# Row tiles and two banks per product in layer 1's first-support stages of a two-layer graph network, with its per-node weights in bursts of two pairs

## The chip, the core and the metric

The kernel runs on one core of a Trainium2 chip. The core has a matrix engine (TensorE, PE in the profile, whose weight loads have a row PEld), a vector engine (VectorE, DVE), a scalar engine (ScalarE, ACT), GpSimd (POOL) and SyncE (SP). Each engine takes its own instructions in program order. TensorE writes only into PSUM, which has eight banks of 512 fp32 values in each of 128 partitions; VectorE and ScalarE read the results from there into SBUF. DMAs are issued from SP, POOL and ACT. The metric is device time in microseconds: the median of three runs, beside one execution taken by the hardware profiler.

## The reference

Two layers, one after the other, on x of shape (8, 2048, 64) with one 2048 x 2048 matrix `adj`; both add a graph convolution to x and normalise over the 64 channels.

```python
# layer 0: supports I, A, 2 A A - I
w = einsum('nd,dkio->nkio', embedding, weight);  b = einsum('nd,do->no', embedding, bias)
x_g = einsum('knm,bmc->bnkc', A_stack, x)
x = layernorm(x + einsum('bnki,nkio->bno', x_g, w) + b)
# layer 1: supports I, A, 2 A A - I, and a fourth made from the embeddings E
apt = softmax(relu(E @ E.T), axis=1)
x_g = einsum('knm,bmc->bknc', stack([I, A, 2*A@A - I, apt]), x)
x = layernorm(x + einsum('bnki,nkio->bno', x_g, weights) + E @ bias_pool)
```

So every node has its own weights, made from a 16-long embedding. All is fp32. The kernel writes an embedding as two parts (a rounded value and what is left), so that a product over 16 embedding rows is one over 64 rows of fast-format (`F32R`) values.

## The kernel before

Nodes are cut into 8 blocks of 256. The work is 40 stages, five phases of eight blocks: A0 and B0 (layer 0: u = A x, then A u with the output), A1 (layer 1: u = A x, the stages that the change is about, numbers 16 to 23), Z1 (softmax support, 24 to 31) and V1 (A u and the output, 32 to 39). The batch and channels of a node make 512 columns.

**Products.** A stage's main work is a product over 2048 rows. Block 0 of A1 is made in the plain way (`straight`, L484): 32 matmuls of 128 contracting rows and 512 columns, 16 for each of two 128-row slabs, two accumulators of one bank each. Blocks 1 to 7 use Strassen's seven products (`strassen`, L504), in the order 1, 4, 7, 2, 6, 5, 3, each of 8 matmuls of 128 rows x 256 columns. An fp32 matmul is two instructions in the profile. Each product has one bank of two in turn (`accumulator`, L480). As a product ends, VectorE adds it to others (L575 to L616); products 1 and 4 are first copied by ScalarE. One matmul of 256 columns counts as one step: a Strassen stage has 56 steps, the plain one 64.

**Everything else is put between the steps.** `put(n, place, job)` plans a job of stage n at a place between 0 and 64, scaled by 56/64 in a stage of 56 steps (L820); the loop from L949 issues a step of the product, then every job that has come due. So order on each engine is fixed by these places. In A1 they are (L886 to L893, L900 to L917):

- `turn(1)` of the block before, at 4: eight transposes of its finished u into one two-bank tile, then four copies by ScalarE;
- `weights` of the block before, in six bursts from 12 to 36 (L336): matmuls of 64 contracting rows (`wst` by `e2`), always two row tiles that work on the two halves h of the array's rows, each with its own bank. Four bursts of six pairs and two of four, two pairs to a two-bank tile. The tiles are then copied to `w`, by ScalarE, but one of each burst by VectorE (L366):

```python
on_dve = k == (0 if self.phase == "V1" else len(made) // 2) and v not in spare and self.n and (v > 16 if self.phase == "A0" else self.phase != "V1" or v0)
```

- `store_c` of the block before, at 24;
- `scores_of_rows` (s=0: two halves, at 38 and 40; s=1: at 57 and 60): two matmuls of 512 columns into one two-bank tile, one VectorE reduction of 1024 columns; `statistics` after each two: small VectorE work and two ScalarE exponentials of 1024 columns. For block 0, s=1 goes into the next stage (14.2 and 19);
- `bias` at 38.5: two small matmuls, then two VectorE additions of 512 columns;
- `apply` of the block before, four times at 43: 32 matmul instructions each in four column tiles of 32, then four VectorE multiply-adds of 256 columns;
- `turn(0, "x")` at 47 (57 in block 0): the same eight transposes for x; two copies by VectorE and two by ScalarE.

All these take a two-bank PSUM tile from `big` (L96), three in turn. With the two accumulators that is all eight banks. Stage 16 also has the tail of layer 0's last block: its `apply` and normalisation, and VectorE's sums of x for Strassen (`sums["A1"].make` at 20, 24 and 32; the fourth in stage 17 at 10). Weights for block 7 of A1 are made in stage 24.

The score matmuls of Z1 (`scores`, `numerators`) contract over 128 rows of `e2`, whose two halves hold the same 64 rows; the upper half of `s1` and `bst` is zero.

SP's queue loads `adj` tiles (four buffers) and `wst` tiles (three), and stores u (L499). POOL's queue stores and loads the rest.

Of the kernel before, what the change touches and what calls it, by code (L numbers as in the profile page):

```python
# [9 lines left out]
F32 = mybir.dt.float32  # L10
F32R = mybir.dt.float32r
AF = mybir.ActivationFunctionType
ALU = mybir.AluOpType
# [35 lines left out]
def two_graph_layers(ctx: ExitStack, tc: tile.TileContext, x, x_t, adj_b, adj_q, layers, out):  # L49
# [33 lines left out]
    ps_acc = ctx.enter_context(tc.tile_pool(name="ps_acc", bufs=1, space=PSUM))  # L83
    ps_big = ctx.enter_context(tc.tile_pool(name="ps_big", bufs=3, space=PSUM))

    in_use = [0]
    in_turn = mybir.DependencyInfo(mybir.DependencyClass.Sync, mybir.DependencyReason.DATA)

    def acc_bank(i):

        return ps_acc.tile([P, BC], F32, tag=f"acc{in_use[0] ^ i}", name="pa")
# [4 lines left out]
    def big(name):  # L96
        return ps_big.tile([P, 2, 512], F32, tag="big", name=name)
# [68 lines left out]
    for li, (e, b) in enumerate(raw):  # L166
        hl = three.tile([P, 8, P], F32R, tag="wst", name="hl")
        eh = halves(e, hl[:, 0:2, :].rearrange("p a n -> p (a n)"), hl[:, 2:4, :].rearrange("p a n -> p (a n)"))
        hb = three.tile([D, 2, C], F32R, tag="f2k", name="hb")
        bh = halves(b, hb[:, 0, :], hb[:, 1, :])  # L170
        ed = dram.tile([4 * D, N], F32, tag=f"ed{li}", name=f"ed{li}")
        for q in range(4):
            pool.dma_start(out=ed[q * D:(q + 1) * D, :].rearrange("d (c n) -> (d c) n", c=NBLK), in_=eh[q % 2])
            pool.dma_start(out=bst[li][q * D:(q + 1) * D, :].bitcast(F32), in_=bh[q // 2])
        estk.append(ed)
# [47 lines left out]
    def load_s1():  # L223
        for q in range(4):
            pool.dma_start(out=s1[q * D:(q + 1) * D, :].bitcast(F32), in_=estk[1][(q // 2) * D:(q // 2 + 1) * D, :])
# [55 lines left out]
    class Stage:  # L281
        def __init__(self, n, phase, j):
            self.n, self.phase, self.j = n, phase, j
            self.li, self.kk = int(phase[1]), int(phase[0] != "A")
            self.half = phase == "B0"
            self.plain = (phase, j) in plain
            self.wide = phase == "Z1" and j >= 2
            self.narrow = phase == "Z1" and j == 1
            self.length = 64 if self.plain else 56
            self.units = C // 2 if self.half else C  # L290
            self.e2 = e2[n % 2]
            self.t = self.sq = None
            self.dev = {}
# [29 lines left out]
        def bias(self):  # L323
            ps = big("pb")
            for s in range(SB):
                pe.matmul(ps[:, s, 0:C], self.e2[:, s * P:(s + 1) * P], bst[self.li], start=True, stop=True)
# [9 lines left out]
        def weights(self, v0, v1):  # L336
# [6 lines left out]
            pairs = list(range(v0, v1))  # L343
            made = [(v, big("pw").rearrange("p h (v n) -> p h v n", n=NB)) for v in pairs[:-1:2]]
# [91 lines left out]
        def turn(self, k, feature=None):  # L436
# [3 lines left out]
            psv = ps.rearrange("p a (q n) -> p (a q) n", n=P)  # L440
            for s in order:
                for q in range(BQ):
                    pe.transpose(psv[:, s * BQ + q, :], slabs[s][:, q * P:(q + 1) * P], ident)
            t = self.features()
            for s in order:
                for par in range(2):
                    src = psv[64 * par:64 * par + 64, s * BQ:(s + 1) * BQ, :]
                    copy(1 if self.phase == "A1" and feature is None else s, t[64 * k:64 * k + 64, s * P:(s + 1) * P, par::2], src.rearrange("p q n -> p n q"))
# [34 lines left out]

        def straight(self, right):  # L484
            accs = [self.accumulator("pu") for _ in range(SB)]
            for m0 in range(0, NJ, 4):
# [4 lines left out]
                for s, m in pairs:  # L491
                    pe.matmul(accs[s], self.a[:, m - m0, s * P:(s + 1) * P], right[m],
                              start=(m == 0), stop=(m == NJ - 1))
                    yield 2
                    if m == NJ - 1:
# [8 lines left out]
        def strassen(self, right):  # L504
# [29 lines left out]
            def times(p):  # L534
                _, left, what = factors[p]
                acc = self.accumulator(f"p{p}")[:, 0:2 * nodes]
                a = (mine[left] if inside else adj.next()).rearrange("p (k n) -> p k n", n=nodes)
                for k in range(k_slab):
                    start, stop = k == 0, k == k_slab - 1
                    if self.kk:  # L540
                        for q in range(2):
                            pe.matmul(acc[:, q * nodes:(q + 1) * nodes], rights[what](k)[:, q * P:(q + 1) * P],
                                      a[:, k, :], start=(start and q == 0), stop=(stop and q == 1))
                            yield nodes / NB
                    else:
                        pe.matmul(acc, a[:, k, :], rights[what](k), start=start, stop=stop)
                        yield 1
                return acc

            def add(dst, a, b, op=ALU.add):  # L550

                if not isinstance(dst, tuple):
# [22 lines left out]
            for p in order:  # L575
# [4 lines left out]
                self.used(factors[p][2])  # L580
                if p == 1:
# [107 lines left out]
        def scores(self, c):  # L689
# [9 lines left out]
            act.activation(p.rearrange("p m n -> p (m n)"), p.rearrange("p m n -> p (m n)"), AF.Exp)  # L699
            self.p[c] = p  # L700

        def numerators(self, t, part):
# [5 lines left out]
            if self.narrow:  # L708
                for h in range(2):
# [5 lines left out]
                    act.activation(p, p, AF.Exp)  # L715
# [4 lines left out]
            act.activation(p, p, AF.Exp)  # L720
# [15 lines left out]
        def scores_of_rows(self, s, h):  # L736
            ps = big("pr")
            for i in range(2):
                at = (2 * h + i) * 512
                pe.matmul(ps[:, i, :], self.e2[:, s * P:(s + 1) * P], s1[:, at:at + 512],  # L740
# [15 lines left out]
        def store_c(self):  # L756
            mine = slice(SB * self.j, SB * self.j + SB)
            dve.tensor_tensor(inv[:, mine, 0], inv[:, mine, 0], inv[:, mine, 1], op=ALU.add)
            dve.reciprocal(inv[:, mine, 0], inv[:, mine, 0])
            for k, a in enumerate((cst, inv[:, :, 0])):  # L760
# [91 lines left out]
    for n, st in enumerate(stages):  # L852
# [3 lines left out]
        cuts = (0, 2, 8, 14, 20, 26, 32) if phase == "V1" and st.j else (0, 6, 12, 16) if st.half else (0, 4, 11, 18, 25, 32) if sevens else (0, 6, 12, 18, 24, 28, 32)  # L856
# [29 lines left out]
        elif phase == "A1":  # L886
            place_weights(n + 1, (12, 15.5, 20.5, 25.5, 32, 36) if 0 < st.j < 7 else (12, 16.5, 21, 25.5, 30, 34.5))
# [61 lines left out]
    for n, st in enumerate(stages):  # L949
        done = 0  # L950
        todo = sorted(plans[n])
# [68 lines left out]
```

## Time and profile before

| what | value |
|---|---|
| timed runs, median (lowest to highest) | 1463.15 us (1461.92 to 1464.17) |
| the profiled execution, first to last instruction | 1460.9 us |
| PE busy | 1439.2 us, 99% |
| PEld busy | 1186.3 us, 81% |
| DVE busy | 971.6 us, 67% |
| ACT busy | 485.0 us, 33% |
| POOL busy | 208.3 us, 14% |
| granted TensorE clock, mean | 0.998 |

The page gives no time of the profiled execution beyond its span, so the span stands for it; the median of the timed runs is 2.25 us above it. A matmul's time in the rows overlaps that of the next one, so the pace is read from the start of one group to the start of the next, or from the chain that ended last, in which the pieces do not overlap. DVE and ACT rows also overlap their neighbours by less than 0.1 us.

### The profile page before, as it was taken

Reading aid. Unit: us, or ns where it says so; the run is one execution under the profiler, and the core shown is the slowest. Engines: PE = TensorE matmul, PEld = TensorE weight load, DVE = VectorE, ACT = ScalarE, POOL = GpSimd, SP = SyncE. Lnnn points to the kernel's source line nnn. Section 1 sums busy time; section 2 is a strip of 40 time slices with the busy share of each in tenths; the row PEclk is TensorE's granted clock in tenths of the full one; section 3 lists DMA queues with packets and bytes.
Section 4 is the critical chain, followed back from the end, with each engine's and each line's share of the span. In section 5 each row is a group of like instructions: output and inputs, shape, how many; then the busy total and the mean of one; then the engine's idle time right before and its main releaser. Section 6 shows DMA issues by size and latency. Waiting matters only on the chain.

```text
span 1460.9 us, 31574 instructions
## 1 busy us (share of the span) xinstructions
PE 1439.2 (99%) x13502; PEld 1186.3 (81%) x13502; DVE 971.6 (67%) x1647; ACT 485.0 (33%) x639; POOL 208.3 (14%) x343
## 2 busy tenths in 40 slices
PE   9999999999999999999999999999999999999997
PEld 4577777778999998568777777799888988888886
DVE  3866666648676666875566676589794566666666
ACT  0444444432211212154544434612110233333332
POOL 5212221110111111211011111011000000000001
PEclk9999999999999999999999999999999999999999
DMA  9788888886666666578787877323313866666662
GB/s 362 275 265 277 283 288 273 269 314 195 209 192 207 200 199 207 158 177 187 201 191 169 216 203 181 51 74 97 86 44 110 251 181 193 188 194 198 190 200 59
DMA packets 88379, 285.50 MB, mean 195 GB/s; under 512 B 14000, under 2 KB 19632, under 8 KB 86640
## 3 DMA queue, kind: packets, MB, share of 16 engines
q1 hardware_dynamic: 55568, 175.13, 40.4%
q0 software_dynamic: 27200, 94.71, 22.0%
q10 hardware_dynamic: 5472, 13.63, 2.8%
q8 instruction: 107, 1.75, 0.5%
q14 instruction: 32, 0.26, 0.0%
HBM read 217.33 MB, written 62.41 MB: 191 GB/s over the span
## 4 chain that ended last, share of the span: by engine, by line
PE 92%; DVE 3%; DMA 3%; issue 1%; ACT 1%; POOL 0%; ACTq 0%; SPq 0%; DVEq 0%
PE pa L43 67%; PE po L43 13%; PE pw L43 8%; DVE acc L43 1%; PE pt L43 1%; DMA wst<-wd 1%; PE ps L43 1%; PE pr L43 1%; DMA t<-t 1%; DVE w L43 1%; DMA a<-in_adj_q 0%; ACT w L43 0%; DMA sd<-sums 0%; DVE t L43 0%; PE pi L43 0%
## 5 line engine op out<-in xcount | busy, mean ns | idle before, releaser
L43 ACT ACTIVATE w<-pw 128x1024 f32<-128x1024 f32 x309 | 304.7, 1029 | 403.2 <-PE pw L43 400.3
L43 DVE SCALAR_TENSOR_TENSOR acc<-po,mask,acc 128x256 f32<-128x256 f32 (+1 forms) x640 | 246.9, 426 | 67.9 <-PE po L43 57.5
L43 DVE COPY w<-pw 128x1024 f32<-128x1024 f32 x127 | 155.5, 1224 | 196.8 <-PE pw L43 196.5
L43 PE MATMUL pa<-a,u 128*128 128x128 f32 (+1 forms) x2048 | 264.0, 285 | 1.3 <-issue 1.2
L43 PEld LDWEIGHTS pa<-a,u 128*128 128x128 f32 x2048 | 245.0, 192 | 13.8 <-issue 3.8
L43 PE MATMUL pa<-x,a 128*128 128x256 f32 (+1 forms) x816 | 238.7, 436 | 0.0
L43 PE MATMUL po<-w,t 128*32 128x256 f32 (+1 forms) x5120 | 206.5, 337 | 7.3 <-issue 6.3
L43 PE MATMUL pa<-u,a 128*128 128x256 f32 x832 | 203.6, 388 | 0.0
L43 PEld LDWEIGHTS pa<-x,a 128*128 128x128 f32 x816 | 150.7, 190 | 60.3 <-issue 38.4
L43 PEld LDWEIGHTS po<-w,t 128*32 128x32 f32 (+1 forms) x5120 | 129.0, 108 | 78.7 <-issue 14.6
L43 PEld LDWEIGHTS pa<-u,a 128*128 128x128 f32 x832 | 151.3, 190 | 29.4 <-issue 5.4
L43 PE MATMUL pw<-e,wst 64*128 64x256 f32 x1680 | 144.4, 295 | 2.2 <-ACT w L43 1.8
L43 PEld LDWEIGHTS pw<-e,wst 64*128 64x128 f32 x1680 | 111.7, 184 | 33.9 <-issue 17.0
L43 PE MATMUL pa<-a,x 128*128 128x128 f32 x768 | 93.0, 277 | 0.0
L43 PEld LDWEIGHTS pa<-a,x 128*128 128x128 f32 x768 | 88.3, 192 | 2.4
L43 PE MATMUL pa<-w,u 128*128 128x256 f32 x384 | 85.8, 379 | 0.0
L43 PE MATMUL pa<-a,w 128*128 128x128 f32 x672 | 81.3, 277 | 0.0
L43 PEld LDWEIGHTS pa<-w,u 128*128 128x128 f32 x384 | 72.0, 190 | 9.3
L43 PEld LDWEIGHTS pa<-a,w 128*128 128x128 f32 x672 | 77.3, 192 | 2.5 <-issue 1.4
L43 ACT ACTIVATE t<-pt 64x512 f32<-64x512 f32 x64 | 40.8, 638 | 76.8 <-DVE t L43 65.2
L43 DVE TENSOR_TENSOR t<-pa,temps 64x256 f32<-64x256 f32 (+1 forms) x130 | 54.0, 415 | 18.5 <-PE pa L43 16.5
L43 POOL DMA_DIRECT2D e<-ed x80 | 42.2, 532 | 168.0 <-PE pw L43 144.3
(129 smaller groups left out, 1271.9 us busy)
## 6 DMA issues: line engine op xcount, KB each, us to landing
wst<-wd SPq DMA_DIRECT2D x108, 512.0 KB, 6.6
a<-in_adj_q SPq DMA_DIRECT2D x90, 512.0 KB, 5.6
a<-sd SPq DMA_DIRECT2D x88, 512.0 KB, 4.6
sd<-a POOLq DMA_DIRECT2D x24, 512.0 KB, 4.6
bx<-bx POOLq DMA_DIRECT2D x32, 256.0 KB, 5.8
acc<-bx POOLq DMA_DIRECT2D x16, 512.0 KB, 7.2
pd<-acc POOLq DMA_DIRECT2D x16, 512.0 KB, 4.6
acc<-pd POOLq DMA_DIRECT2D x16, 512.0 KB, 8.4
```

The lines of the kernel that those rows point to most:

```text
L43: return self._tc.keep_in_program_order(f(*args, **kwargs))
```

## The change

In A1 stages (`by_rows`) each matmul of 128 contracting rows becomes two of 64, one for each half of the array's rows, with a bank for each half. A product then has two banks, which are added as it is evacuated: a ScalarE copy of one and a VectorE addition of the other, or two VectorE additions. Transposes, bias and row scores are cut in the same two row tiles. Products use two pairs of banks in turn, and `big` has two tiles in turn in these stages instead of three. Weights of blocks 0 to 6 are made in 16 bursts of two pairs (one two-bank tile each) instead of six bursts. The rule on L366 is as before. For the row tiles, the upper halves of `s1` and of layer 1's `bst` are filled as well, by four more DMAs each; scores over 128 rows thus come out doubled, and the exponential's scale of 0.5 and a doubled `cst` undo that.

```diff
+    banks = [psum.tile([P, 2, BC], F32, tag=f"ps{i}", name=f"ps{i}") for i in range(4)]
     def acc_bank(i):
-        return ps_acc.tile([P, BC], F32, tag=f"acc{in_use[0] ^ i}", name="pa")
+        return banks[0][:, in_use[0] ^ i, :]
     def big(name):
-        return ps_big.tile([P, 2, 512], F32, tag="big", name=name)
+        turn_of[0] += 1
+        return banks[2 + turn_of[0] % 2] if by_rows[0] else banks[1 + turn_of[0] % 3]
...
-            pool.dma_start(out=bst[li][q * D:(q + 1) * D, :].bitcast(F32), in_=bh[q // 2])
+            for r in range(0, P if li else 64, 64):
+                pool.dma_start(out=bst[li][r + q * D:r + (q + 1) * D, :].bitcast(F32), in_=bh[q // 2])
...
     def load_s1():
-        for q in range(4):
+        for q in range(8):
...
+            self.by_rows = phase == "A1"
...
         def bias(self):
-                pe.matmul(ps[:, s, 0:C], self.e2[:, s * P:(s + 1) * P], bst[self.li], start=True, stop=True)
+                r = slice(64 * s, 64 * s + 64) if self.by_rows else slice(0, P)
+                pe.matmul(ps[:, s, 0:C], self.e2[r, s * P:(s + 1) * P], bst[self.li][r, :], start=True, stop=True)
...
         def turn(self, k, feature=None):
+            if self.by_rows:
+                for s in order:
+                    for q in range(BQ):
+                        for h in range(2):
+                            r = slice(64 * h, 64 * h + 64)
+                            pe.transpose(ps[:, h, (s * BQ + q) * 64:(s * BQ + q + 1) * 64],
+                                         slabs[s][r, q * P:(q + 1) * P], ident[r, 64 * h:64 * h + 64])
...
+        def pair_of_banks(self):
+            in_use[0] ^= 1
+            return [banks[in_use[0]][:, h, :] for h in range(2)]
+        def both(self, accs, cut, left, right, **flags):
+            if not self.by_rows:
+                pe.matmul(cut(accs), left, right, **flags)
+                return
+            for h, acc in enumerate(accs):
+                r = slice(64 * h, 64 * h + 64)
+                pe.matmul(cut(acc), left[r], right[r], **flags)
...
         def straight(self, right):
-            accs = [self.accumulator("pu") for _ in range(SB)]
+            accs = [self.pair_of_banks() if self.by_rows else self.accumulator("pu") for _ in range(SB)]
+                    if m == NJ - 1 and self.by_rows:
+                        act.copy(self.slabs[s], accs[s][0])
+                        dve.tensor_tensor(self.slabs[s], self.slabs[s], accs[s][1], op=ALU.add)
...
         def strassen(self, right):
+                if self.by_rows:
+                    upper, lower = acc
+                    if p in (1, 4, 7):
+                        to = {1: w1, 4: w4, 7: v}[p]
+                        act.copy(to, upper)
+                        add(to, to, lower)
+                    elif p == 6:
+                        add(w1, upper, w1)
+                        add(w1, w1, lower)
+                        add(v, v, w1)
+                        add(c10, v, w4, ALU.subtract)
+                    else:
+                        for dst, a in {2: ((c00, w1),), 5: ((w1, w1), (c11, v)), 3: ((c01, w1),)}[p]:
+                            add(dst, upper, a)
+                            add(dst, lower, dst)
+                    continue
...
-            act.activation(p, p, AF.Exp)
+            act.activation(p, p, AF.Exp, scale=0.5)
...
         def scores_of_rows(self, s, h):
-                pe.matmul(ps[:, i, :], self.e2[:, s * P:(s + 1) * P], s1[:, at:at + 512],
+                r = slice(64 * i, 64 * i + 64)
+                pe.matmul(ps[:, i, :], self.e2[r, s * P:(s + 1) * P], s1[r, at:at + 512],
...
         def store_c(self):
+            dve.tensor_scalar(cst[:, mine], cst[:, mine], 2.0, None, op0=ALU.mult)
...
-        cuts = (0, 2, 8, 14, 20, 26, 32) if phase == "V1" and st.j else (0, 6, 12, 16) if st.half else (0, 4, 11, 18, 25, 32) if sevens else (0, 6, 12, 18, 24, 28, 32)
+        cuts = (0, 2, 8, 14, 20, 26, 32) if phase == "V1" and st.j else (0, 6, 12, 16) if st.half else range(0, 33, 2) if phase == "A1" and st.j < 7 else (0, 4, 11, 18, 25, 32) if sevens else (0, 6, 12, 18, 24, 28, 32)
...
         elif phase == "A1":
-            place_weights(n + 1, (12, 15.5, 20.5, 25.5, 32, 36) if 0 < st.j < 7 else (12, 16.5, 21, 25.5, 30, 34.5))
+            if st.j < 7:
+                place_weights(n + 1, [12 + 1.6 * i for i in range(16)])
+            else:
+                place_weights(n + 1, (12, 16.5, 21, 25.5, 30, 34.5))
...
     for n, st in enumerate(stages):
+        by_rows[0] = st.by_rows
```

## The prediction

> **What bounds the kernel now.** I read the page's busy times first, then the windows of the A1 stages, then the chain of work that ended last inside one stage, then VectorE's timeline there.
>
> ```profile
> span 1460.9 us, 31574 instructions
> PE 1439.2 (99%) x13502; PEld 1186.3 (81%) x13502; DVE 971.6 (67%) x1647; ACT 485.0 (33%) x639; POOL 208.3 (14%) x343
> ```
>
> PE is never idle, so what comes off its path comes off the time, as long as nothing else takes over. By windows, stage 19 (columns: busy us of PE, PEld, DVE, ACT, POOL):
>
> ```profile
> 691.93:733.30 41.37, 41.37 (x331) 32.27 (x330) 26.09 (x50) 18.96 (x26) 5.36 (x9) 1.00 0.78 194
> ```
>
> Stages 18 to 22 each take 41.4 us; VectorE fills 26.1 of it. The chain in it (start, us, what; pieces follow one another):
>
> ```profile
> 711.42 3.02 PE pa L43 x14
> 714.44 0.91 PE pw L43 x12
> 715.35 1.49 PE pa L43 x6
> 716.84 0.91 PE pw L43 x12
> 717.75 1.92 PE pa L43 x8
> ...
> 728.78 0.65 PE pw L43 x8
> 729.44 1.06 PE pa L43 x4
> 730.50 0.47 PE pr L43 x2
> ...
> 733.38 0.77 PE po L43 x9
> ```
>
> pa is the product: 3.02/14 = 0.216 us an instruction, 0.432 a step. Eight instructions after a weight burst take 1.92, which is 0.19 too many, and the burst (0.91 for six pairs, 0.66 for four, so 0.125 a pair) has 0.16 that belongs to no pair: 0.35 lost per burst; 0.46 if a pair takes only 0.107, half of an fp32 instruction's 0.216. pr, also fast format but in 128 rows, pays nothing (0.47 for 2 x 0.216), so the loss goes with the row tiles. VectorE and ScalarE in the same window:
>
> ```profile
> 714.30 0.37 ACT L43 COPY temps<-pa 128x256 f32<-128x256 f32 x1
> 714.92 1.94 ACT L43 ACTIVATE w<-pw 128x1024 f32<-128x1024 f32 x2 [0.24 <-PE pw L43]
> ...
> 715.15 1.22 DVE L43 COPY w<-pw 128x1024 f32<-128x1024 f32 x1 [5.56 <-PE pw L43]
> 717.55 1.23 DVE L43 COPY w<-pw 128x1024 f32<-128x1024 f32 x1 [1.18 <-PE pw L43]
> 720.38 1.23 DVE L43 COPY w<-pw 128x1024 f32<-128x1024 f32 x1 [1.61 <-PE pw L43]
> 723.65 1.22 DVE L43 COPY w<-pw 128x1024 f32<-128x1024 f32 x1 [1.77 <-PE pw L43]
> 724.79 0.41 DVE L43 TENSOR_TENSOR temps<-pa,temps 128x256 f32<-128x256 f32 x1
> ```
>
> VectorE takes one of a burst's two or three tiles and then waits; ScalarE takes the others.
>
> **What PE gains.** Six bursts' loss goes: 2.1 to 2.8, I take 2.5. Four pr pairs run side by side: 4 x 0.21 = 0.84. Turns: 16 loads and half-long matmuls instead of 8; between 0.87 saved in a stage (two turns halved) and 0.87 lost (loads one behind another); I take 0, as no row is nearer to one end. Products in row tiles: the half-stage applies before (64 rows x 32 columns, 128 instructions of 0.107 in 2.0 us) show that two row tiles work at once in fp32, so a step stays 0.432; upper bound 0.48, by the pair's 0.12 against 0.107. PE alone would need 41.4 - 3.3 = 38.1.
>
> **What VectorE gets.** The rule on L366 gives it tile number len(made) // 2. A burst of two pairs has one tile, so that is number 0: VectorE copies all 16, ScalarE none. Before it was 6 and 10. Start to start a copy takes 1.15 (723.65 to 724.79). Plus 10 x 1.15 = 11.5; products have 15 additions for 9, 6 x 0.41 = 2.5; doubling cst 0.2. VectorE goes to 26.1 + 14.2 = 40.3, more than PE's 38.1, and 18.4 of it comes as one train in a stretch where PE has 15.0 us of work today (714.44 to 729.44). With two tiles in turn PE can be two bursts ahead, no more.
>
> The Trainium skill, "TensorEngine Tiling (Array Packing)", section "PSUM Bottleneck", says that tiling speeds up TensorE but not the evacuation of PSUM, and advises using both engines for it. This speaks against the change as written: with copies shared 6 and 10 as in the rows above the stage would be PE's 38.1, with all on VectorE it is the chain below; the code decides for the second.
>
> **The chain of a changed stage**, 0 = its first burst (PE step 11), additions 0.37, or 0.5 where one needs the one before (724.79 row to the next at 725.31), 0.2 where PE changes to or from column tiles:
> - VectorE's queue holds P1's addition ahead of burst 0's copy; it waits for ScalarE's copy of P1, behind the turn's copies. That makes the start 1.0 instead of 0.55. Train: 1.0 + 16 x 1.15 + P4's and P7's additions 0.75 + store_c 0.6 = 20.75. Burst 15 waits for copy 13, at 18.45; PE is at step 32 at 18.75 (15.0 before).
> - Step 34 at 19.6, first pr 19.9, bias waits for copy 15: 20.95. Step 35 at 21.4; the second pr waits for the first's tile, which VectorE frees after P2's additions (21.6) at 22.8: 23.1. Step 38 at 24.4.
> - apply: VectorE needs 4 x 0.49 = 1.97 for each (16 rows in 7.89 us), PE 1.76. With two tiles the third and fourth wait: PE 26.4, 28.15, 30.3, 32.25 (25.98 before); VectorE 28.45, 30.4, 32.4, 34.4.
> - VectorE then: P6 36.4, x copies 37.7, P5 39.5, pr 40.7 and 41.9, statistics 42.3, P3 43.15. PE: step 42 at 34.2, turn, step 50 at 38.5, two pr, step 56 at 41.6, four steps to 43.3, the turn of u (its slab is ready at 43.15), seven steps: next first burst at 47.2.
> - ScalarE: exponentials 42.3 to 44.8, turn copies to 47.3, P1's copy 47.7, addition 48.1: the 1.0 that I began with.
>
> So 47.2 against 41.4: **+5.8 a stage**. Lower bound +4.0 (P1's wait gone, 0.9; dependent additions as cheap as others, 0.4; half of the turn's gain, 0.5). Upper +8.0 (step 0.48, at most 56 x 0.048 = 2.7, of which the train hides 21 steps' share and other waits some: 1.0; copies at their full 1.225: 1.2).
>
> **Stage 16** has a stall of its own. VectorE is behind by its sums of x:
>
> ```profile
> 614.24 2.02 DVE L43 TENSOR_TENSOR u<-x 128x1792 f32<-128x1792 f32 x1
> 616.17 1.22 DVE L43 TENSOR_SCALAR_CACHE_REDUCE sq<-pr 128x1024 f32<-128x1024 f32 x1
> 617.32 0.08 DVE L43 DVE_READ_ACCUMULATOR sq<-pr 128x1 f32 x1
> 617.32 1.28 DVE L43 TENSOR_TENSOR bx<-x,pb 128x512 f32<-128x512 f32 x2
> 618.51 1.22 DVE L43 TENSOR_SCALAR_CACHE_REDUCE row<-pr 128x1024 f32<-128x1024 f32 x1
> ```
>
> PE makes the second pr at 611.28 in the third tile. With two tiles it waits for the first reduction, to 617.4: 6.1, and all of the stage's later steps stand behind it on PE. Less 2 x 0.21 for pr: **+5.8** (bounds +4 and +6.5).
>
> **Stages 17, 23, 24.** In 17 the fourth sum of x (2.28) stands ahead of copy 0 and two reductions and statistics (2.8) stand in the train: 5.1, of which the stage pays 3.1 now (22.0 from first burst to apply, against 18.94): +5.8 + 2.0 = **+7.8** (5 to 10.5). In 23 three `scores` in 128 rows now change the tiling twice each (3 x 0.4) and put 3 x 0.61 on a VectorE that is late: **+7.8** (4 to 11); stage 24 starts behind VectorE's rest: **+1** (0 to 2).
>
> **Costed at nothing.** Four more bst DMAs on POOL at the start push the load of the first e2 from 18.97 by 4 x 0.53; it lands 5.8 later, 24.8 to 26.9, and its first user, a bias, runs at 27.07; without that cover 1 us. Four more s1 DMAs (stage 4), the exponential's scale and the halves' own DMAs: POOL is 14% busy; s1 is used 400 us later. The wst loads come with the same tiles. store_u waits on SP for P3's later sum, with adj loads behind it: four buffers, each 3.5 us of PE, cover 3 us. bias, store_c and load_acc on POOL come some 4 us later; acc is needed 30 us on. The last two slabs of stage 16 get a ScalarE copy and an addition (0.6 + 0.7) for one copy: four steps and the turn's place cover it. Other phases keep their banks: two accumulators and three tiles.
>
> **Sum.** 5.8 + 7.8 + 5 x 5.8 + 7.8 + 1 = 51.4 on the span of 1460.9: 1512.3. The median of the runs is 2.25 above that span: 1514.6, say 1514. Bounds: 4 + 5 + 20 + 4 + 0 = 33 gives 1496; 6.5 + 10.5 + 40 + 11 + 2 = 70 gives 1533. About 3 us (0.2%) is what a measurement can tell from nothing.
>
> **Rivals.**
> - *Faster: the copies don't bind.* PE's 38.1 sets the stage: 7 x -3.3 + 5.8 = -17, 1446. For it VectorE's 40.3 would have to be under 38.1, so three copies or more would have to leave it; against it L366. 3%.
> - *VectorE binds only by its sum.* If its work spread evenly, a stage is 40.3 to 41.4, and stage 16's stall is left: -8 + 6 to +6, 1461 to 1469. Against it: two tiles cannot spread a train of 18.4 over a stage. 5%.
> - *The loss at bursts stays* (not the tiling's but each burst's own). 16 x 0.35 on PE, which in the train waits anyway (21 x 0.432 + 16 x 0.6 = 18.7, just under the train); outside it nothing changes: +0 to 1 a stage, 1514 to 1522. Against it pr's 0.47. 8%.
> - *Row tiles take turns.* A step is 0.864, a stage 38.1 + 24.2 = 62.3, stage 16 +28: 7 x 21 + 28 + 6, near 1640. Against it the applies in 64 rows. 4%.
>
> **How the numbers follow.** My forecast has 80%, its own range 1496 to 1533. Rivals one, two and four leave 12% outside; for sizes off in the chain I widen to 1490 to 1540. Faster: the first rival and a fifth of the second, 4%; same: 2%; slower 94%.
>
> **What would show it.** A1 windows near 47 us with VectorE near 40 busy; 112 VectorE copies of w in stages 17 to 23, back to back, and PE waiting for them in the bursts; a PE wait of 6 us for `sq` in stage 16; steps at 0.43 with no extra 0.19 after bursts. Wrong if ScalarE makes w copies there, if steps stretch, or if VectorE idles inside the bursts.

## The result, and the profile after

The changed kernel takes **1820.74 us** (median, 1816.64 to 1824.85) where the kernel before, beside it on the same chip, takes 1462.54 us (1461.67 to 1464.17). The ratio is **1.2452, with a 95% interval of 1.2425 to 1.2479**. The forecast was 1514 us, 1490 to 1540: the direction was right and the size badly wrong. The profiled execution spans 1815.4 us, 354.5 more than the 1460.9 before. The first two lines of its page:

```profile
span 1815.4 us, 33506 instructions
...
PE 1516.1 (84%) x14478; PEld 1184.8 (65%) x14478; DVE 1067.8 (59%) x1767; ACT 421.9 (23%) x578; POOL 212.0 (12%) x351
```

PE's busy time rose by 77 us, and its idle time from 22 us to 299. No other engine is full either. So the kernel is now a chain of waits, and the question is where they lie. A part of the added busy time is a lower clock: the granted clock was 0.50 in stretches of 3.4 or 6.8 us that add up to 78 us, 48 of them outside A1, besides the last 8 us of the span; the kernel before has it only in its last 7 us. At half speed that is at most 39 of the 77 us.

To place them, both traces are cut at the same instruction: VectorE's first multiply-add of each block's `apply`. That of A1's block 0 lies in stage 17, and so on. The table gives the time at which the kernel passes the mark of the last block of a phase, in us from the start of the span.

| stretch, up to the mark of | before | after | longer by |
|---|---|---|---|
| A0, last block | 332.9 | 427.7 | 94.8 |
| B0, last block (in stage 16) | 589.9 | 747.4 | 62.7 |
| A1, block 0 (in stage 17) | 652.6 | 824.1 | 14.1 |
| A1, blocks 1 to 6 (stages 18 to 23) | 901.4 | 1110.8 | 37.9 |
| A1, block 7 (stage 24) | 948.3 | 1161.2 | 3.5 |
| Z1 and V1, to the end of the span | 1460.9 | 1815.4 | 141.6 |

The stages that the change rewrites lost 55.5 us in all, close to the 51.4 of the forecast. The other 299 us were lost in phases that the change seems to leave alone (that PE's idle time is also 299 us is chance: it has A1's waits in it, and the 299 lost here have some busy time). By windows (columns as in the prediction: length, then busy us of PE, PEld, DVE, ACT, POOL, granted clock, DMA share, GB/s), first one interval of B0 and one of A1 in the changed kernel:

```profile
548.10:589.60 41.50, 34.24 (x533) 31.51 (x519) 22.55 (x55) 6.90 (x9) 4.99 (x8) 1.00 0.53 170
871.90:919.70 47.80, 42.76 (x466) 30.47 (x462) 39.43 (x67) 9.64 (x17) 5.36 (x8) 0.96 0.65 167
```

and the same interval of B0 in the kernel before:

```profile
427.40:460.70 33.30, 32.83 (x534) 31.16 (x527) 22.58 (x55) 6.90 (x9) 4.98 (x8) 1.00 0.68 211
```

In B0 every engine does the same work as before, in 41.5 us for 33.3, at a full clock. Nearly all that is new is PE's idle time, 7.3 us for 0.5. PE's timeline in a later interval of B0 of the changed kernel (start, us, what, then in brackets the idle time before it and who ended it):

```profile
601.37 3.84 PE L43 MATMUL ps<-a,u 128*128 128x128 f32 x32 [1.13 <-DVE t L43]
606.82 3.84 PE L43 MATMUL ps<-a,w 128*128 128x128 f32 x32 [1.61 <-DVE t L43]
611.94 3.84 PE L43 MATMUL ps<-a,u 128*128 128x128 f32 x32 [1.28 <-DVE t L43]
```

and the kernel before, where the same products follow one another without a gap:

```profile
441.58 3.74 PE L43 MATMUL pa<-a,w 128*128 128x128 f32 x32
445.16 5.08 PE L43 MATMUL pa<-a,u 128*128 128x128 f32 x44
```

VectorE's timeline in the changed kernel shows what PE waits for: the additions that evacuate the product just finished.

```profile
605.25 0.76 DVE L43 TENSOR_TENSOR temps<-ps,temps 128x256 f32<-128x256 f32 x2 [1.21 <-PE ps L43]
605.92 0.84 DVE L43 TENSOR_TENSOR t<-ps,temps 64x256 f32<-64x256 f32 x2
```

A product of 32 instructions ends at 605.2, the four additions run from 605.25 to 606.76, and the next product starts at 606.82. It writes the other bank, yet it waits: in the packed trace, its first weight load and its first matmul wait for a semaphore that VectorE raises as the fourth addition ends. Over the whole span, PE's waits of the changed kernel (for whom, us in all, times, longest):

```profile
PE ps L43 <- DVE t L43: 116.6, 76, 5.8
PE ps L43 <- DVE u L43: 36.6, 26, 2.6
PE ps L43 <- ACT temps L43: 31.0, 45, 2.1
PE ps L43 <- ACT w L43: 28.3, 24, 1.3
PE ps L43 <- DVE w L43: 25.9, 69, 2.4
PE ps L43 <- DVE sq L43: 14.4, 8, 6.5
PE ps L43 <- DVE temps L43: 13.1, 22, 1.2
```

Before, the longest entry of this list was

```profile
PE po L43 <- issue: 6.3, 8, 1.4
```

`t`, `u` and `temps` are destinations of evacuated products. ScalarE's `w`, 24 times, all in A0, are copies of weights: there a burst of seven pairs puts its odd pair into the accumulator bank that is not in use. The entries `DVE w` and `DVE sq` are A1's own, those that the prediction spoke of. The line of the diff behind the first kind is in the head of the kernel: the two accumulators, until now two tiles of one bank, have become `banks[0][:, 0, :]` and `banks[0][:, 1, :]`, two halves of one tile, and all phases use them.

### The profile page after: what moved, and what is told of

Its sections match the earlier page's. It is cut to its first block, busy times and chain, and to the rows that moved or that the text cites. A ratio compares the mean times of both kernels' runs of the same rounds, so it can differ in the third digit from the quotient of the medians.

```text
span 1815.4 us, 33506 instructions
## 1 busy us (share of the span) xinstructions
PE 1516.1 (84%) x14478; PEld 1184.8 (65%) x14478; DVE 1067.8 (59%) x1767; ACT 421.9 (23%) x578; POOL 212.0 (12%) x351
## 5 line engine op out<-in xcount | busy, mean ns | idle before, releaser
L43 ACT ACTIVATE w<-ps 128x1024 f32<-128x1024 f32 (+1 forms) x263 | 245.1, 992 | 536.4 <-PE ps L43 465.2
L43 DVE COPY w<-ps 128x1024 f32<-128x1024 f32 x197 | 233.6, 1220 | 209.6 <-PE ps L43 209.6
L43 PE MATMUL ps<-a,u 128*128 128x128 f32 (+1 forms) x2048 | 279.4, 291 | 65.5 <-DVE t L43 50.8
L43 DVE SCALAR_TENSOR_TENSOR acc<-ps,mask,acc 128x256 f32<-128x256 f32 (+1 forms) x640 | 247.8, 426 | 121.8 <-PE ps L43 81.4
L43 PEld LDWEIGHTS ps<-a,u 128*128 128x128 f32 x2048 | 250.5, 194 | 90.5 <-DVE t L43 59.2
L43 PE MATMUL ps<-x,a 64*128 64x256 f32 (+3 forms) x1216 | 248.1, 431 | 30.1 <-ACT w L43 14.7
L43 PE MATMUL ps<-u,a 64*128 64x256 f32 (+1 forms) x1280 | 220.5, 399 | 45.2 <-DVE u L43 25.0
L43 PE MATMUL ps<-w,t 128*32 128x256 f32 (+1 forms) x5120 | 213.3, 343 | 3.9 <-DVE acc L43 3.1
L43 PEld LDWEIGHTS ps<-u,a 64*128 64x128 f32 (+1 forms) x1280 | 153.7, 194 | 76.6 <-DVE u L43 28.1
L43 PE MATMUL ps<-e,wst 64*128 64x256 f32 x1728 | 164.3, 306 | 20.2 <-DVE w L43 19.1
L43 PEld LDWEIGHTS ps<-w,x 128*128 128x128 f32 x288 | 57.5, 204 | 31.9 <-DVE t L43 19.9
L43 DVE TENSOR_TENSOR t<-ps,temps 64x256 f32<-64x256 f32 (+1 forms) x130 | 53.9, 415 | 41.3 <-PE ps L43 39.5
```

The source lines that it names most:

```text
L43: return self._tc.keep_in_program_order(f(*args, **kwargs))
```

## The experiments

Each diff is against the kernel named with it; ratios are against the kernel before, run beside it, with their 95% intervals. "A stage" below is the interval between the marks of two neighbouring blocks of A1 in the stages 18 to 23: 41.4 us before, 47.8 after.

**The two accumulators as two tiles again**, against the changed kernel. All else of the change stays.

```diff
-    banks = [psum.tile([P, 2, BC], F32, tag=f"ps{i}", name=f"ps{i}") for i in range(4)]
+    accs01 = [psum.tile([P, BC], F32, tag=f"pa{i}", name=f"pa{i}") for i in range(2)]
+    banks = [None] + [psum.tile([P, 2, BC], F32, tag=f"ps{i}", name=f"ps{i}") for i in range(1, 4)]
...
-        return banks[0][:, in_use[0] ^ i, :]
+        return accs01[in_use[0] ^ i]
...
-            return [banks[in_use[0]][:, h, :] for h in range(2)]
+            return [banks[1][:, h, :] for h in range(2)] if in_use[0] else list(accs01)
```

> The changed kernel with one edit: the two accumulator banks of the other phases are two tiles again instead of two halves of one; all else stays, the banks' places too. Theory A (one tile makes the matmuls into one bank wait until the other bank's result has been read, so each product outside A1 starts only after the last one's evacuation): A0, B0, Z1 and V1 go back to the kernel before, A1 stays as changed, 47.8 us a stage. Of the 354.5 us between the two spans 55 (A1) stay: 1516 of span, timed 1513 to 1525. Theory B (the loss outside A1 comes from which banks are used side by side, or from something else in the change): it stays near 1820, or at least above 1600.

Measured: **1520.22 us** (1519.52 to 1520.83), 1.0379 (1.0362 to 1.0397): 300 us back by an edit that issues the same matmuls and additions. Two windows, B0 and A1:

```profile
428.30:461.70 33.40, 32.76 (x534) 31.09 (x519) 22.51 (x55) 6.90 (x9) 4.96 (x8) 1.00 0.70 211
715.40:763.20 47.80, 42.68 (x466) 30.41 (x462) 39.46 (x67) 9.63 (x17) 5.34 (x8) 0.96 0.71 175
```

B0 is back at 33.4, and the stage of A1 is unchanged at 47.8. PE's longest waits are now those of A1 alone:

```profile
PE ps L43 <- DVE w L43: 26.9, 70, 2.4
PE ps L43 <- DVE sq L43: 14.6, 9, 6.5
PE ps L43 <- issue: 6.0, 10, 0.8
```

This run is the change that the prediction worked out, and it took 1520.2 for the 1514 forecast.

**The converse: the kernel before, with its two accumulators in one tile.** Nothing else is changed.

```diff
+    both_accs = ps_acc.tile([P, 2, BC], F32, tag="accs", name="pa")
...
-        return ps_acc.tile([P, BC], F32, tag=f"acc{in_use[0] ^ i}", name="pa")
+        return both_accs[:, in_use[0] ^ i, :]
```

> The kernel before with one edit: its two accumulator banks become two halves of one tile; no row tiles, no other bursts, same banks. Theory A: the other phases lose what they lost in the changed kernel (94.8 in A0, 62.7 in B0, 141.6 from Z1 on: 299), and A1's seven products a stage, here also in these two banks, lose about as much as in V1, 8 us a stage: 1462 + 299 + 8 x 8 = 1825, 1790 to 1850. Theory B: 1463, within 5.

Measured: **1860.62 us**, 1.2704 (1.2683 to 1.2724). That is above the 1790 to 1850 expected. The size outside A1 is the changed kernel's (a B0 interval takes the same 41.5 us), but A1 lost 92.6 us from the mark in stage 16 to that in stage 24 (451.0 for 358.4), with stages of 52.0 to 55.3: 11 to 14 each where some 8 had been expected. A part of that is the clock: three of the six stages take 52.0; the two that take 53.7 each have one stretch of 3.4 us at a granted clock of 0.50, and the one that takes 55.3 has two. So such a stretch costs 1.7 us here. PE's waits name the same evacuations, `u` (A1's slabs) more than in the changed kernel:

```profile
PE pa L43 <- DVE t L43: 115.8, 75, 5.8
PE pa L43 <- DVE u L43: 81.8, 55, 3.7
PE pa L43 <- ACT temps L43: 45.6, 59, 2.1
```

So the one tile is enough for the loss without any of the rest of the change, and taking it back removes the loss with all of the rest in place. (Here the tile is made once and not for each product; so are the two tiles of the run before, which have no such loss.) In A1 itself the change does not suffer from it, since a product there has a whole tile, and the next one the other tile.

The kernel's banks are the same 512 values per partition in all four kernels, and PE never wrote the bank that VectorE was reading. The Trainium skill, "PSUM — Partial Sum Buffer", section "PSUM bank collisions raise a hardware error", asks for guarding PSUM by bank and quadrant, by bank in the simple version. These runs agree that a wait by bank is enough for this kernel's results, and they price the coarser wait by tile at 300 us here.

**What sets the A1 stage: who copies the weights.** From here on the kernels have two accumulator tiles. The first gives every second burst's tile to ScalarE, against the two-tile kernel.

```diff
-                on_dve = k == (... len(made) // 2) and v not in spare and self.n and (...)
+                on_dve = k == (... len(made) // 2) and v not in spare and self.n and (...) and (len(made) > 1 or v0 % 4 == 0)
```

> Two accumulator tiles again, and in A1's bursts of two pairs the copies of w go to VectorE and ScalarE in turn, 8 each. Theory C (VectorE's train of 16 copies sets these stages): the train falls to 8 x 1.15 + 1.4, under PE's own work of the stretch; a stage falls from 47.8 to between 40 and 43, in all 1516 - 7 x 6 = 1475, 1462 to 1488. Theory D (two tiles in turn instead of three hold PE back whoever copies): a stage stays at 46 to 48, 1503 to 1518.

Measured: **1483.56 us**, 1.0129 (1.0113 to 1.0144), 36.7 less than with all copies on VectorE. The stage falls from 47.8 to 42.5, VectorE's busy time in it from 39.5 to 31.0:

```profile
704.70:747.10 42.40, 39.53 (x462) 29.93 (x458) 31.02 (x58) 17.54 (x26) 5.34 (x8) 1.00 0.79 201
```

So the stage was bound by VectorE's train of copies, as the prediction said. Of the 5.3 us, some 1.7 are the clock: a stretch at 0.50 that each of these stages had around the start of its applies (shown in the section on the prediction) went with the waits. What is left over the 41.4 of before is not PE's need, which is 39.5.

**Bursts of four pairs instead of two**, against the two-tile kernel, so that each burst has two tiles and the old rule shares them.

```diff
-range(0, 33, 2) if phase == "A1" and st.j < 7
+range(0, 33, 4) if phase == "A1" and st.j < 7
...
-                place_weights(n + 1, [12 + 1.6 * i for i in range(16)])
+                place_weights(n + 1, [12 + 3.2 * i for i in range(8)])
```

> Two accumulator tiles again, and A1's weights in eight bursts of four pairs (two tiles each), so that by the unchanged rule ScalarE copies the first tile and VectorE the second; 8 copies each as in the kernel with shared copies, in another order. Theory C: 39 to 42 a stage, 1455 to 1480. Theory D: 46 to 48, 1503 to 1518. If single bursts spread over the steps are worth something in themselves, it is slower than the kernel with shared copies; if not, the same or faster.

Measured: **1487.75 us** (1485.58 to 1490.44), 1.0157 (1.0142 to 1.0172), outside the 1455 to 1480 expected. Four of the six stages take 41.1 to 42.1, as expected, but two take 47.6 and 44.4. In the longest, PE stands still ahead of an `apply`, and the trace names nobody:

```profile
755.70 4.48 PE L43 MATMUL ps<-w,t 128*32 128x256 f32 x46 [4.41 <-issue]
```

A stretch of 3.4 us at a clock of 0.50 follows it. The likeliest cause is a transfer on the DMA queue of kind `instruction` (q8 on the page): one ended at 754.27, 1.4 us before PE went on. In all the traces together PE has 58 such unnamed stops of over 0.6 us behind the first 60 us, and in 55 of them such a transfer ended 1.2 to 1.6 us before PE went on, though a run has only 107 to 114 of these transfers. No run takes the transfer away, so this is argued and not shown. The stage of 44.4 has no long stop, and stays open.

**Bursts of two pairs without the row tiles**, against the kernel before, with the copies shared as above.

```diff
-... and (v > 16 if self.phase == "A0" else self.phase != "V1" or v0)
+... and (v > 16 if self.phase == "A0" else self.phase != "V1" or v0) and (len(made) > 1 or v0 % 4 == 0)
...
-            place_weights(n + 1, (12, 15.5, 20.5, 25.5, 32, 36) if 0 < st.j < 7 else (12, 16.5, 21, 25.5, 30, 34.5))
+            place_weights(n + 1, [12 + 1.6 * i for i in range(16)] if st.j < 7 else (12, 16.5, 21, 25.5, 30, 34.5))
```

(and `range(0, 33, 2)` in the cuts, as in the change.)

> The kernel before (no row tiles for products, three tiles, one bank a product) with the change's 16 bursts of two pairs in stages 17 to 23, copies to VectorE and ScalarE in turn. Theory H (each burst between matmuls of 128 rows pays 0.35 to 0.46 for the change of tiling): ten more bursts cost 3.5 to 4.6 a stage, 1463 + 7 x 4 = 1491, 1485 to 1497. Rival (the loss belongs to the pairs, or to something other than the tiling): within 5 of 1463.

Measured: **1489.23 us**, 1.0173 (1.0158 to 1.0188), as expected. The stage takes 45.4 and PE is busy in all of it. The chain of work that ended last:

```profile
722.26 0.63 PE pa L43 x2
722.88 0.43 PE pw L43 x4
723.32 1.06 PE pa L43 x4
724.38 0.43 PE pw L43 x4
724.81 0.63 PE pa L43 x2
```

A burst takes 0.43, and the one step behind it 0.63 where a step takes 0.432: a burst of two pairs costs 0.63. In the changed kernel the same burst, between steps that are row tiles too, costs 0.24:

```profile
844.01 0.59 PE L43 MATMUL ps<-e,wst 64*128 64x256 f32 x4
844.44 0.59 PE L43 MATMUL ps<-u,a 64*128 64x256 f32 x4
844.68 0.59 PE L43 MATMUL ps<-e,wst 64*128 64x256 f32 x4
```

From one burst's start to the next is 0.67, of which the step between is 0.432. So going into row tiles and out again costs 0.39 a burst, and it goes away when the neighbours have the same tiling. That also prices the ten extra bursts at 3.9 us of the stage, 41.4 + 3.9 = 45.3 for the 45.4 measured.

**Row tiles from block 1 on only**, against the shared copies.

```diff
-            self.by_rows = phase == "A1"
+            self.by_rows = phase == "A1" and j > 0
...
-                r = slice(64 * s, 64 * s + 64) if self.by_rows else slice(0, P)
+                r = slice(64 * s, 64 * s + 64) if self.li else slice(0, P)
```

> The kernel with two accumulator tiles and shared copies, and block 0 of A1 (stage 16) again in 128 rows with one bank an accumulator and three two-bank tiles; its row scores and bias stay in row tiles. Theory F (stage 16's 6.5 us are the second row score's wait for one of only two tiles): they go, and about 1.5 come for changes of tiling around scores and bias: 1483.6 - 5 = 1478.5, 1476 to 1481. Theory G (VectorE is late there in any case, and another wait takes the place): 1482 to 1485.

Measured: **1480.55 us**, 1.0112 (1.0095 to 1.0129). The interval from the mark in stage 16 to that in stage 17 fell from 73.4 to 68.5, and 1.6 came back up to the mark in stage 24. Stage 16's own wait in the changed kernel, which this edit takes away, is here on PE's timeline:

```profile
767.96 0.59 PE L43 MATMUL ps<-bst,e 64*128 64x64 f32 x2
775.09 0.80 PE L43 MATMUL ps<-s,e 64*128 64x512 f32 x2 [6.53 <-DVE sq L43]
```

**Three jobs moved**, against that: the bias earlier, the turn's copies of u shared by both engines, the last sum of x earlier.

```diff
-                    copy(1 if self.phase == "A1" and feature is None else s, dst, src)
+                    copy(1 if self.phase == "A1" and feature is None and not self.by_rows else s, dst, src)
...
-    put(17, 10, sums["A1"].make, 1)
+    put(17, 2, sums["A1"].make, 1)
...
-            put(n, 48 if n == 0 else 36 if st.li == 0 else 38.5, st.bias)
+            put(n, 48 if n == 0 else 36 if st.li == 0 else 6 if st.by_rows else 38.5, st.bias)
```

> As the kernel with block 0 whole, and three jobs moved off VectorE's crowded places: bias from 38.5 to 6, two of the four copies of the turned u to VectorE (ScalarE then reaches P1's copy earlier), the fourth sum of x from place 10 to 2 of stage 17. If what is left above the kernel before is waits for two tiles behind VectorE's queue (0.6 at the bursts' start, 0.7 at the second score, 2.4 in stage 17), stages 18 to 22 fall from 42.5 to about 41.0 and stage 17 by 2: 1467, 1459 to 1474. If it is PE's own work in row tiles, it stays at 1476 to 1480.

Measured: **1474.79 us**, 1.0072 (1.0057 to 1.0087), 0.8 above the interval expected. Most of the gain is in stage 17 (68.5 to 64.3); the stage went from 42.5 to 42.1 only. The three jobs were not tried one by one.

**Row tiles in stages 17 to 22 only, bursts spread further**, against that.

```diff
-            self.by_rows = phase == "A1" and j > 0
+            self.by_rows = phase == "A1" and 0 < j < 7
...
-            if st.j < 7:
-                place_weights(n + 1, [12 + 1.6 * i for i in range(16)])
+            if st.j < 6:
+                place_weights(n + 1, [8 + 1.95 * i for i in range(16)])
...
-            for s, h, place, later in ((0, 0, 38, 0), (0, 1, 40, 0), (1, 0, 57, 14.2), (1, 1, 60, 19)):
+            for s, h, place, later in ((0, 0, 38, 0), (0, 1, 40, 0), (1, 0, 57, 1), (1, 1, 60, 5.5)):
...
-            put(n, 48 if n == 0 else 36 if st.li == 0 else 6 if st.by_rows else 38.5, st.bias)
+            put(n, 48 if n == 0 else 36 if st.li == 0 else 53 if st.by_rows else 38.5, st.bias)
```

(Block 6 gets its six bursts back with this, and block 0's later `statistics` move along with its scores.)

> Row tiles and bursts of two pairs in stages 17 to 22 only (16 and 23 as before, but for scores and bias in row tiles), two accumulator tiles, shared copies, two of the four u-turn copies on VectorE, bias at 53, block 0's later scores at 1 and 5.5 of stage 17, and the 16 bursts spread from 8 to 37.25 instead of 12 to 36. With two tiles a pair of bursts can't come faster than a copy and its hand-offs, about 1.9 us as in the kernel with shared copies (PE's 1.7 plus its waits); spread, PE has 1.95 of its own work for two bursts. Theory D' (after the sharing, two tiles' turn-around is what is left): stages 18 to 22 at 40 to 41, 1455 to 1466, at or a little under the kernel before. Rival (PE's own work in row tiles is no less than before): 41.5 and more, 1467 to 1475.

Measured: **1471.08 us**, 1.0032 (1.0022 to 1.0043), where 1455 to 1466 was expected. Block 7's interval came back to 46.5 (52.5 in the kernel that it is made from), but the stage is at 42.5 to 42.9 with PE busy for 39.34 of it, and the rest has a place:

```profile
715.49 0.50 PE L43 MATMUL ps<-e,wst 64*128 64x256 f32 x4 [1.54 <-DVE t L43]
```

The second burst waits for a tile that VectorE holds for two copies of the turn, and those had waited for ScalarE, on VectorE's timeline:

```profile
713.95 1.40 DVE L43 COPY t<-ps 64x512 f32<-64x512 f32 x2 [2.99 <-ACT t L43]
```

ScalarE does two exponentials of the row scores first, each of 1024 columns.

**The same with the bursts close again** (`[12 + 1.6 * i for i in range(16)]`).

> The same with the bursts at the change's places, 12 to 36. Theory D': 0.8 to 1.5 a stage slower than the spread one, 1461 to 1472. Rival: the same time as the spread one, within 2.

Measured: **1472.06 us**, 1.0046 (1.0027 to 1.0064). The interval holds the other kernel's 1.0032: how far the bursts are spread makes no difference that these runs can tell.

**The exponentials moved behind the turn**, against the kernel of the stages 17 to 22: all four of the turn's copies of u are on ScalarE again, and the later half's two exponentials go to places 11 and 17 of the next stage.

```diff
-                    copy(1 if self.phase == "A1" and feature is None and not self.by_rows else s, dst, src)
+                    copy(1 if self.phase == "A1" and feature is None else s, dst, src)
...
-            put(*((n, 62) if st.j else (n + 1, 7)), st.statistics, 1)
+            put(*((n, 62) if st.j else (n + 1, 7)), st.statistics, 1, 0 < st.j < 6)
+            if 0 < st.j < 6:
+                put(n + 1, 11, st.exponentials, 1, 0)
+                put(n + 1, 17, st.exponentials, 1, 1)
```

> As the kernel with rows in stages 17 to 22, but all four copies of the turned u on ScalarE again, and the two exponentials of a block's later scores not at the end of its stage but at 11 and 17 of the next one, so that ScalarE's queue has the turn copies and P1's copy ahead of them. If the 1.5 us that PE waits at the bursts' start comes from ScalarE's queue (exponentials, then turn copies, then P1's copy, then VectorE's addition, then its first copy of w), stages 18 to 22 fall by 1.0 to 1.5 from 42.6: 1465, 1459 to 1468, even with the kernel before or a little under it. If the wait only moves into the bursts, where ScalarE is then missing for 2.4 us, it stays at 1469 to 1473.

Measured: **1463.61 us**, 0.9999 (0.9989 to 1.0009): no difference to the kernel before. The stage takes 41.3, and the wait at the second burst is down to 0.18:

```profile
713.22 0.50 PE L43 MATMUL ps<-e,wst 64*128 64x256 f32 x4 [0.18 <-ACT t L43]
...
720.92 0.50 PE L43 MATMUL ps<-e,wst 64*128 64x256 f32 x4 [0.48 <-DVE w L43]
```

The wait at 720.92 comes from VectorE, which in this stage waited three times for ScalarE's copy of a product's first bank (a line of VectorE's waits):

```profile
DVE temps L43 <- ACT temps L43: 2.4, 3, 1.4
```

**That copy on VectorE too**, against the last one, with the later scores moved to 58.2 and 60.8.

```diff
-                        act.copy(to, upper)
+                        dve.tensor_copy(to, upper)
...
-            for s, h, place, later in ((0, 0, 38, 0), (0, 1, 40, 0), (1, 0, 57, 1), (1, 1, 60, 5.5)):
+            for s, h, place, later in ((0, 0, 38, 0), (0, 1, 40, 0), (1, 0, 58.2, 1), (1, 1, 60.8, 5.5)):
```

> As the kernel with later exponentials, but the first bank of products 1, 4 and 7 is copied by VectorE instead of ScalarE (before it, VectorE's addition, with copies of w queued behind it, waited for ScalarE's copy, itself queued behind a copy of w or an exponential), and the later scores of a block are put one step on (58.2 and 60.8). If these hand-overs are what leaves PE waiting in the bursts (0.48 and 0.35) and at the score (0.49), stages 18 to 22 fall from 41.3 by 0.8 to 1.3 and the kernel to 1457, 1455 to 1460, under the kernel before. If VectorE's own load is what PE waits for, three more copies of 0.4 on it make it the same or slower: 1462 to 1468.

Measured: **1455.5 us** (1453.78 to 1457.15), 0.9942 (0.9929 to 0.9956), 0.6% below the kernel before. VectorE now has more work than in the last one (32.2 for 31.1), and the stage is shorter, 40.0, of which PE is busy for 39.1:

```profile
688.80:728.70 39.90, 39.14 (x462) 29.95 (x458) 32.23 (x61) 16.47 (x24) 5.36 (x8) 1.00 0.77 200
```

PE's waits for VectorE's copies of `w` in the stage above, 0.48 and 0.35 us, are gone, and so is one of 0.49 ahead of a row score. The first two name the copies that stood behind the product's addition; the third can be the scores' move. The two edits were not run apart.

Of the 8.9 us by which its span (1452.0) is under that of before, 2.6 lie ahead of the mark in stage 16, in layer 0; the two-tile kernel showed 1.3 there, and the cause is open. The six stages themselves give 6.4 (242.4 for 248.8), and the intervals on both sides of them 1.6; Z1 and V1 take 1.7 more.

## Why the prediction was right and wrong

**The step that failed** is under "Costed at nothing": "Other phases keep their banks: two accumulators and three tiles." They keep two banks, but not two tiles, and a matmul into one half of a tile waited for the readers of the other. The diff's first lines show it, `banks[0][:, in_use[0] ^ i, :]` in `acc_bank`, which all phases call; I read them as a renaming. It cost 299 of the 354.5 us (94.8 + 62.7 + 141.6), 300 by the pair of runs. There are 175 Strassen products outside A1 (42 in A0, 49 in B0, 28 in Z1, 56 in V1), so it is some 1.7 us for each, if the plain products' share is counted with them: about what the evacuation takes that had lain beside the next product. That also shows where a trace of before could have bounded it. VectorE's additions behind each product were in it, and the only question was whether the next product would stand behind them. I did not ask it, and neither the range nor a rival had the case.

**The sum for A1 came out, in part by luck.** By the same marks: stages 16 and 17, forecast 5.8 + 7.8 = 13.6, measured 14.1 in the changed kernel and 16.3 with two tiles. For stages 18 to 23 the forecast has 6 x 5.8 = 34.8 up to the mark; its 2 us for stage 23's three `scores` lie behind that mark. Measured: 37.9 in both kernels, and 3.5 and 3.9 up to the mark in stage 24, where the forecast has 2 + 1.

But the sum has no term for the clock. In each of these stages the granted clock was 0.50 for 3.4 us, around the start of the applies. In the stage shown above, by windows:

```profile
914.90:918.40 3.50, 3.50 (x28) 1.91 (x28) 2.01 (x5) 1.32 (x3) 2.15 (x4) 0.51 0.86 344
```

VectorE then waits for PE, on its timeline:

```profile
919.68 1.52 DVE L43 SCALAR_TENSOR_TENSOR acc<-ps,mask,acc 128x256 f32<-128x256 f32 x3 [2.70 <-PE ps L43]
```

The last twelve product instructions ahead of the applies take 2.44 us here and 1.39 in the kernel with shared copies, whose stages have no such stretch. At the 1.7 us that a stretch cost in the converse kernel, the stage would be some 46.1 without it (an estimate), where 47.2 was forecast. In the two-tile kernel's rows the chain reaches the second row score 22.6 us after its first burst (forecast 23.1) and the first apply at 25.9 (24.6); from VectorE's first multiply-add to the next first burst it takes 19.9 (20.7). So the clock and a chain put somewhat too long offset each other. Stages 16 and 17 have 10.2 us at 0.50, up to 5.1 of what they lost. The terms:

- The stage: forecast 47.2, measured 47.8. VectorE's busy time: forecast 40.3, measured 39.43.
- All 16 copies on VectorE: the page counts 197 VectorE copies of `w` for 127 before, which is 70 more, ten for each of seven stages. They come as the train that was forecast, in pieces of 2.4 to 6.9 us between other work, on VectorE's timeline of a changed stage:

```profile
892.82 0.42 DVE L43 TENSOR_TENSOR temps<-temps,ps 128x256 f32<-128x256 f32 x1 [4.67 <-ACT temps L43]
893.16 4.61 DVE L43 COPY w<-ps 128x1024 f32<-128x1024 f32 x4
897.69 0.41 DVE L43 TENSOR_TENSOR temps<-temps,ps 128x256 f32<-128x256 f32 x1
898.01 4.61 DVE L43 COPY w<-ps 128x1024 f32<-128x1024 f32 x4
...
902.86 2.35 DVE L43 COPY w<-ps 128x1024 f32<-128x1024 f32 x2
905.13 0.41 DVE L43 TENSOR_TENSOR temps<-temps,ps 128x256 f32<-128x256 f32 x1
905.46 6.88 DVE L43 COPY w<-ps 128x1024 f32<-128x1024 f32 x6
```

  The first line also has the wait with which the chain began: P1's addition stands ahead of the first copy, and waits for ScalarE's copy of P1.
- The step, kept at 0.432: measured 3.02 us for 28 instructions, seven steps, so 0.431 (lines below). *Row tiles take turns* is refuted.
- The loss at a burst, 0.35 to 0.46: 0.39, and it goes with the tiling, not with the burst. *The loss at bursts stays* is refuted.
- The turns, which I took at 0 between 0.87 saved and 0.87 lost: a turn of u takes 0.50 (below, 840.62 to 841.12) for 0.87 before, so two turns save about 0.74 of PE's time. In a stage bound by VectorE that bought nothing.

```profile
837.60 3.19 PE L43 MATMUL ps<-x,a 64*128 64x256 f32 x28
840.62 0.66 PE L43 MATMUL ps<-ident,u 64*128 64x64 f32 x16
841.12 1.95 PE L43 MATMUL ps<-x,a 64*128 64x256 f32 x16
```

- PE alone, 38.1: the kernels with shared copies show 39.1 to 39.5 busy. The saving is thus 1.9 to 2.3 a stage and not 3.3. The bursts are short: counted from one PE instruction's start to the next and without waits, products and bursts take 28.9 to 29.4 us for 29.8 before, so 0.5 to 1.0 came of the 2.5. Row scores gave 0.9 to 1.2 (forecast 0.84), turns 0.5 to 0.8 (forecast 0); the applies take 0.4 more.
- Stage 16's wait for `sq`, forecast 6.1: measured 6.53.

**The rivals.** *The copies don't bind* is wrong for the change as written: with all 16 on VectorE the stage is 47.8, with 8 it is 42.5, and only with the waits of VectorE and ScalarE for each other taken out as well does it come down to 40.0, near PE's 39.1. *VectorE binds only by its sum* is wrong too: busy for 39.4, it let a stage take 47.8. The advice of the Trainium skill, "TensorEngine Tiling (Array Packing)", section "PSUM Bottleneck", that both engines should evacuate PSUM, which the prediction weighed against the change, agrees with these runs: sharing the copies gave 36.7 us. But the last experiment goes the other way for three copies a stage, of the first banks of products 1, 4 and 7: VectorE had waited 2.4 us a stage for ScalarE to make them, and makes each itself in 0.4. How much of that run's gain is theirs, and how much the scores' move, was not tried.

## What to carry to other kernels

When a change rewrites how buffers are allocated, it changes every stage that uses them, also those whose code is untouched: ask of each pair of buffers whether they are still two tiles, because the program waits for a tile as a whole, and two halves of one tile gave no double buffering here (+300 us). When the size of a group changes, follow every rule that counts its members (`len(made) // 2`): here it moved ten copies a stage to one engine, and the sum of that engine's work was a worse guide to the time than the order in which it was queued. A gain on the busiest engine shows only after the others' waits for one another are gone: of the row tiles' 2 us a stage, 1.4 came out when the exponentials were moved behind the turn and a product was no longer passed between two engines. And read the granted clock by stage before taking a sum that came out for a mechanism that was right.

## What was not expected of the hardware

- Cutting a transpose of 128 rows into two of 64 in two row tiles makes it faster, though it doubles the instructions and the loads: 16 in 0.50 us for 8 in 0.87.
- A burst in row tiles costs PE 0.39 us more between matmuls of 128 rows than between matmuls that are row tiles too (0.63 for 0.24).
- A granted clock of 0.50 came in stretches of 3.4 or 6.8 us in the kernels whose PE had to wait; in the converse kernel a stretch of 3.4 us cost 1.7 us (stages of 53.7 with one and 55.3 with two, for 52.0).
- The wait by tile is not the hardware's: it is a semaphore wait that the program was built with, as the trace has it at 606.82.
